# Broadcast rows, saved node states and summed attributes of a graph network moved by two or four DMA engines instead of up to sixteen

## The chip, the cores and the metric

The kernel runs on one core of a Trainium2 chip. The metric is the device time of one execution in microseconds; lower is better. The core has TensorE (PE, with its weight loads PEld), VectorE (DVE), ScalarE (ACT), GpSimd (POOL) and SyncE (SP). SP, ACT and POOL also issue transfers, and all transfers are carried by the same 16 DMA engines.

## The reference

12,500 nodes with 128 features and 200,000 edges pass through two graph networks. `x` enters a gated message layer, is added and normalised; the result passes through three layers of a second network, which sum over a node's edges the neighbour's features and the edge's encoded attributes, and it is added and normalised again.

```python
# layer 0: messages by destination, then a GRU
src_h = h[src] @ W_msg.T + b_msg
msg = src_h + edge_embed[clip(edge_type)]
messages = segment_sum(msg, dst)
x = layernorm(x + gru(messages, h))
# layers 1 to 3: the edges by source, and their attributes
ee = ea @ enc_w + enc_b
agg = segment_sum(concat(x[ei[1]], ee), ei[0])
h = relu(batchnorm(agg @ w1 + b1)) @ w2 + b2
# at the end
x = layernorm(x + h)
```

## The kernel before

**Preparation (0 to about 1250 us).** The edges are sorted twice on chip by two keys, and lists of places are made. Nothing of the change is used there except two writes of summed attributes.

**Four layers.** Nodes are split into NB = 98 blocks of P = 128. `layer(i, pace)` loops over the 98 output blocks `o`. For every block there is a row of slots: 32 slots for each of the 98 other blocks (CW = 3136 numbers in bfloat16), where each number says which of the 128 nodes of that other block belongs to the slot. Layers 0 and 1 use the whole row. Layers 2 and 3 use the first 72 blocks of it (IC*SL = 2304 numbers) and fetch the other rows by indirect gathers.

One block `o` goes through these steps:

- `slots_of` (L1507) loads the row into the tile `inr`, the same row into every one of the 128 partitions, with one DMA from SP. In layers 0 and 1 one row is loaded at a time (784 KB into SBUF); in layers 2 and 3 two rows (1152 KB). There is one buffer for `inr`, so the next load waits until the last block of the tile has been compared.
- `one_hots` makes two one-hot operands on DVE: `g` from `inr` (L1519), and `s` from the columns of the edges (L1524, four pieces). It runs one block ahead; `g` and `s` have two buffers each.
- TensorE picks rows with `g` (L1615), ACT copies them out of PSUM as `e` (L1621, L1624; DVE takes a third in layers 0 and 1, L1622), and TensorE adds them up with `s` into `acc` (L1565; gathered rows by L1570). `acc` has one buffer.
- `finish` adds `acc` in three parts to `s` on DVE (L1581 to L1583), which frees `acc`; for every two blocks `gru` (layer 0) or `gin` (layers 1 to 3) does the dense part, with L1462 on PE and L1467 on DVE (L1477 in layer 3).

The orders of the instructions on DVE, ACT and PE inside the layers are chosen by a scheduler when the program is built, and are then fixed: every engine runs its list in order. POOL's list is written by hand.

**Attributes.** `attributes` runs beside layers 0 and 1. For each block POOL issues 17 indirect gathers of 128 rows of 64 bytes (L718). `add_up` then copies the gathered tile on ACT (L738) and DVE (L739), which wait for the last of the 17. Summed attributes of seven blocks are written to DRAM as `eaT` (102 rows, L777), and `gin` reads them back as `cT` (L1433). The normalised output of layer 0 is written to DRAM as `x1` (L1357) and read back as `xx` in layer 3 (L1436).

**Rows in DRAM.** `Slots.decode` writes, during layer 0, `sl` into `inrow0` (the rows for layer 0) and `dl` into `inrow1` (the rows for layers 1 to 3). The program's access patterns for the loads before are 128 partitions on both sides:

```python
inrow = [dram(f"inrow{i}", (NB, n), BF16) for i, n in enumerate((CW, CW))]
inr = inr.rearrange("p (b c) -> p b c", c=n)
nc.sync.dma_start(inr, inrow[a][None, o:o + per, :n].to_broadcast([P, per, n]))
```

Of the kernel before, what the change touches and what calls it, by code (L numbers as in the profile page):

```python
# [9 lines left out]
BF16 = mybir.dt.bfloat16  # L10
# [8 lines left out]
H = 128  # L19
# [4 lines left out]
P = 128  # L24
NB = -(-N // P)
NPAD = NB * P
NW = NB + 2
H3 = 3 * H
SL = 32
CW = NB * SL  # L30
# [17 lines left out]
IC = 72  # L48
# [25 lines left out]
E6 = 6 * EA  # L74
# [14 lines left out]
def gnn_kernel(ctx: ExitStack, tc: tile.TileContext, x, xx, src, dst, ea, et, w_msg, w_ihT, w_hhT, b_msg,  # L89
# [4 lines left out]
    def dram(name, shape, dtype=F32):  # L94
        return nc.dram_tensor(name, shape, dtype, kind="Internal").ap()
# [4 lines left out]
    tables = [dram(f"table{i}", (P * NW, H3), BF16) for i in range(4)]  # L100
    ovf = [dram("ovf0", (P * NW, H + NTX))] + [dram(f"ovf{i}", (P * NW, H)) for i in (1, 2, 3)]
    ovfe = dram("ovfe", (P * NW, EA))
    x1d = dram("x1", (P, NB, H))

    def by_node(t, b0, n):

        return t.rearrange("(p b) f -> p b f", b=NW)[:, b0:b0 + n, :]

    inrow = [dram(f"inrow{i}", (NB, n), BF16) for i, n in enumerate((CW, CW))]
    outrow0 = dram("outrow0", (NB, CW), BF16)  # L110
    typerow = dram("typerow", (NB, CW), BF16)
    eaTd = dram("eaT", (E6, NPAD), BF16)

    const = ctx.enter_context(tc.tile_pool(name="const", bufs=1))
    psa = ctx.enter_context(tc.tile_pool(name="psa", bufs=1, space=PSUM))
# [250 lines left out]
    XC = 7  # L366
# [361 lines left out]
    def add_up(b, at):  # L728
        if b % XC == 0:
            owns.append(owp.tile([P, XC, EA], F32, name="own"))  # L730
            nc.sync.dma_start(owns[-1], by_node(ovfe, b, XC))
        own = owns[-1][:, b % XC, :]
        oh = eop.tile([P, P, WC], BF16, name="eoh")
        a3 = attr3[b % 2]
        for f0 in range(0, P, P // 2):

            if f0 == 0:
                A.copy(a3[:, :, 1:EA], at)  # L738
                V.tensor_sub(at, at, a3[:, :, 1:EA])  # L739
            else:  # L740
                A.copy(a3[:, :, EA:EA + DE], at)
                V.tensor_sub(a3[:, :, EA + DE:], at, a3[:, :, EA:EA + DE])
            V.tensor_tensor(oh[:, f0:f0 + P // 2, :], iotas[:, f0:f0 + P // 2, :WC],  # L743
                            slcol[:, b, None, :].to_broadcast([P, P // 2, WC]), op=OP.is_equal)
            yield
        early = sorting[-1]
        ps = psa.tile([P, 512], F32, name="acc") if early else psd.tile([P, 512], F32, name="d")
        for t in range(WN):
            T.matmul(ps[:, :EW], oh[:, :, t], a3[:, t, :], start=(t == 0), stop=(t == WN - 1))  # L749
        if early:  # L750
            yield
        V.tensor_add(own, own, ps[:, :EA])
        V.tensor_add(own[:, 1:], own[:, 1:], ps[:, EA:EA + DE])
        V.tensor_add(own[:, 1:], own[:, 1:], ps[:, EA + DE:EW])
        yield
        if early:
            yield
            yield
        if b % XC < XC - 1:
            return  # L760
        own = owns[-1]
        own6 = ow6.tile([P, XC, 6, EA], BF16, name="own6")
        times = lambda n: own[:, :, None, :].to_broadcast([P, XC, n, EA])
        V.tensor_copy(own6[:, :, 0:3, :], times(3))
        V.tensor_sub(own, own, own6[:, :, 0, :])
        yield
        V.tensor_copy(own6[:, :, 3:5, :], times(2))
        V.tensor_sub(own6[:, :, 5, :], own, own6[:, :, 3, :])
        yield
        pt = psa.tile([P, 1024], BF16, name="acc") if early else psd.tile([P, 1024], BF16, name="d")  # L770
        for k in range(XC):
            T.transpose(pt[:E6, k * P:(k + 1) * P], own6[:, k, :, :].rearrange("p a b -> p (a b)"), identb)
        if early:
            yield
        eT = ow6.tile([E6, XC * P], BF16, name="ownT")
        A.copy(eT, pt[:E6, :XC * P])
        nc.sync.dma_start(eaTd[:, (b - XC + 1) * P:(b + 1) * P], eT)  # L777
        summed.extend(range(b - XC + 1, b + 1))
        yield

# [278 lines left out]
    class Slots:  # L1059
# [15 lines left out]
        def decode(self, c):  # L1075

            if c >= CHUNKS:
                return
            b0, n = c * CB, min(CB, NB - c * CB)
            cells, bs, m = self.cells.pop(c), slice(b0, b0 + n), n * SL  # L1080
            ci = cells.bitcast(I32)[:, :m]
            tile_of = lambda name, d=BF16, pool=self.pool: pool.tile([NB, CB * SL], d, name=name)
            valid, ty, sm, dm = (tile_of(x) for x in ("valid", "ty", "sm", "dm"))
            sl, dl = (tile_of(x, pool=self.two) for x in ("sl", "dl"))
            fi = tile_of("fi", I32)
            as3 = lambda t: t[:, :m].rearrange("p (b s) -> p b s", s=SL)
            by_dst = lambda d: d.rearrange("d (s k) -> s d k", k=SL)
            V.tensor_tensor(as3(valid), iota[:NB, None, :SL].to_broadcast([NB, n, SL]),
                            cnt[:, bs, None].to_broadcast([NB, n, SL]), op=OP.is_lt)

            def field(to, shift, mask):
                V.tensor_scalar(fi[:, :m], ci, shift, mask, op0=OP.logical_shift_right, op1=OP.bitwise_and)
                V.tensor_scalar(to[:, :m], fi[:, :m], sgn[:NB], off[mask][:NB], op0=OP.mult, op1=OP.add)

            field(sl, 11, 127)
            nc.sync.dma_start(by_dst(inrow[0])[:, bs, :], as3(sl))
            yield
            field(dl, 4, 127)
            V.scalar_tensor_tensor(dm[:, :m], valid[:, :m], -200.0, dl[:, :m], op0=OP.mult, op1=OP.add)
            field(ty, 0, 15)  # L1100
            nc.sync.dma_start(inrow[1][:, b0 * SL:(b0 + n) * SL], dl[:, :m])
            V.scalar_tensor_tensor(sm[:, :m], valid[:, :m], -200.0, sl[:, :m], op0=OP.mult, op1=OP.add)
            yield
            ps = psd.tile([P, 512], F32, name="d")
            for k in range(n):
                for x, t in enumerate((dm, ty)):
                    for r in range(4):
                        T.matmul(ps[r * SL:(r + 1) * SL, (x * CB + k) * NTL:(x * CB + k + 1) * NTL],
                                 t[:, k * SL:(k + 1) * SL], sel[:, r, :], start=True, stop=True, skip_group_check=True)
                T.matmul(ps[k * SL:(k + 1) * SL, 256:256 + NB], sm[:, k * SL:(k + 1) * SL], identb[:NB, :NB],  # L1110
                         start=True, stop=True, skip_group_check=True)
            for x, to in enumerate((outcol[0], typecol)):
                A.copy(to[:, bs, :NTL], ps[:, x * CB * NTL:(x * CB + n) * NTL].rearrange("p (b t) -> p b t", b=n))
            m = n * SL
            A.copy(outcol[1][:m, :, CELL + c], ps[:m, 256:256 + NB])
            yield
# [220 lines left out]
    def layernorm(y, b0, n, final):  # L1337
        st = lnp.tile([P, GL, 6], F32, name="ln_st")
        mv = lnp.tile([P, GL, 2], F32, name="ln_mv")
        for k in range(n):  # L1340
            V.bn_stats(st[:, k, :], y[:, k, :])
            V.bn_aggr(mv[:, k, :], st[:, k, :])
            if k % 4 == 3:
                yield
        rstd = lnp.tile([P, GL], F32, name="ln_r")
        rsqrt(rstd[:, :n], mv[:, :n, 1], [P, n], lnp)
        yield
        for k in range(n):
            V.tensor_scalar(y[:, k, :], y[:, k, :], mv[:, k, 0:1], rstd[:, k:k + 1],
                            op0=OP.subtract, op1=OP.mult)  # L1350
            if k % 2:
                if not final:
                    split3(y[:, k - 1:k + 1, :], 1, b0 + k - 1, k == n - 1)
                yield
        if not final:
            nc.sync.dma_start(by_node(ovf[1], b0, n), y[:, :n, :])
        nc.sync.dma_start((out if final else x1d)[:, b0:b0 + n, :], y[:, :n, :])  # L1357

    group = {}

# [64 lines left out]
    def gin(i, b0, s):  # L1425
        yield
        k4 = b0 % 4
        if k4 == 0:
            m = min(4, NB - b0)
            while len(summed) < b0 + m:  # L1430
                next(attr)
            four["eT"] = dq.tile([E6, 4 * P], BF16, name="cT")
            nc.sync.dma_start(four["eT"][:, :m * P], eaTd[:, b0 * P:(b0 + m) * P])  # L1433
            if i == 3:
                four["xx"] = dq.tile([P, 2, 2, 2 * H], F32, name="xx")
                nc.sync.dma_start(four["xx"][:, 0].rearrange("p a (b f) -> p (a b) f", b=2)[:, :m, :], x1d[:, b0:b0 + m, :])  # L1436
            else:
                four["o"] = dq.tile([P, 4, H], F32, name="n")
        eT = four["eT"][:, k4 * P:(k4 + 2) * P]
# [45 lines left out]
    def layer(i, pace):  # L1485
# [16 lines left out]
        def slots_of(o):  # L1502

            n = nb * SL
            inr = rp.tile([P, 2 * IC * SL], BF16, name="inr")[:, :per * n]
            inr = inr.rearrange("p (b c) -> p b c", c=n)
            nc.sync.dma_start(inr, inrow[a][None, o:o + per, :n].to_broadcast([P, per, n]))  # L1507
            inrs.append(inr)

        def one_hots(o):  # L1510

# [197 lines left out]
```

## Time and profile before

| | |
|---|---|
| median of 3 runs | 6211.23 us (6205.5 to 6216.66) |
| the profiled execution | 6211.41 us |
| its span, first to last instruction | 6209.6 us |
| mean granted TensorE clock | 0.888 |
| PE busy | 4981.5 us (80%) |
| DVE, ACT, POOL busy | 3730.2, 3722.9, 3328.5 us |
| row loads: layers 0 and 1 | 196 of 784 KB |
| row loads: layers 2 and 3 | 98 of 1152 KB |

The stretches of the span are: preparation to 1250 us, layer 0 to about 2880, layer 1 to 4235, layer 2 to 5210, layer 3 to the end. A line number such as L1507 is a line of the kernel before; in the changed kernel the same lines stand 9 to 11 lines further down. Busy shares are means over a stretch; what a change is worth is read from what ends the waits there.

### The profile page before, as it was taken

How to read it: one execution, taken by the hardware profiler on the slowest of the kernel's cores; microseconds unless marked ns; L12 is line 12 of the kernel's file. 1: busy time of each engine (PE TensorE's matmuls, PEld its weight loads, DVE VectorE, ACT ScalarE, POOL GpSimd, SP SyncE). 2: the span in 40 equal slices, each digit the busy share in tenths (PEclk: the TensorE clock that was granted, in tenths of full speed). 3: DMA queues.
4: the chain of work that ended last, by engine and by line, in shares of the span. 5: the costliest groups of instructions: out<-in, count | busy, mean ns of one | idle time of the engine just before them, and what ended most of it. 6: DMA issues, size and time to landing. Idle time of an engine off the chain costs nothing. (4 is left out here: it accounts for less than half of the span.)

```text
span 6209.6 us, 129682 instructions
## 1 busy us (share of the span) xinstructions
PE 4981.5 (80%) x50669; PEld 2867.1 (46%) x50669; DVE 3730.2 (60%) x9301; ACT 3722.9 (60%) x5300; POOL 3328.5 (54%) x4109
## 2 busy tenths in 40 slices
PE   3872431148888888898899999958999998999999
PEld 3872121124444444443455555534555555555555
DVE  9977777656766766666566656634444443444444
ACT  7770221025665656565677777736777776777776
POOL 1004777356665666665566666663555553655553
PEclk9755555568999999999999999979999999999999
DMA  1001210022222322224222223214444445444443
GB/s 71 22 1 32 84 38 8 11 53 77 82 81 80 96 79 84 81 86 146 83 89 93 91 88 98 89 44 163 143 139 139 139 139 164 145 137 137 136 137 103
DMA packets 278104, 575.34 MB, mean 93 GB/s; under 512 B 74269, under 2 KB 169897, under 8 KB 276835
## 3 DMA queue, kind: packets, MB, share of 16 engines
q1 hardware_dynamic: 158946, 416.84, 19.2%
q0 software_dynamic: 105920, 116.17, 8.1%
q10 hardware_dynamic: 12616, 33.99, 1.6%
q8 instruction: 397, 6.50, 0.4%
q14 instruction: 225, 1.84, 0.1%
HBM read 478.02 MB, written 88.73 MB: 91 GB/s over the span
## 5 line engine op out<-in xcount | busy, mean ns | idle before, releaser
L1624 ACT CAST e<-g 128x1152 bf16<-128x1152 f32 (+1 forms) x2156 | 2260.1, 1061 | 746.7 <-PE g L1615 668.6
L1615 PE MATMUL g<-x,g 128*32 128x384 bf16 x33320 | 1954.8, 335 | 156.1 <-ACT e L1624 80.4
L718 POOL DMA_INDIRECT eat<-in_ea,eidcol x1666 | 1768.9, 1062 | 543.2 <-issue 448.9
L1565 PE MATMUL acc<-e,s 128*128 128x384 bf16 (+3 forms) x8428 | 1978.4, 349 | 89.5 <-DVE s L1583 58.6
L1565 PEld LDWEIGHTS <-s 128*128 128x128 bf16 (+1 forms) x8428 | 1090.2, 155 | 869.8 <-issue 643.8
L1541 POOL DMA_INDIRECT x<-table,rowcol x980 | 974.3, 994 | 918.5 <-PE acc L1570 728.0
L1615 PEld LDWEIGHTS <-g 128*32 128x32 bf16 x33320 | 698.4, 96 | 1077.4 <-issue 851.6
L1621 ACT CAST e<-g 128x768 bf16<-128x768 f32 x784 | 627.8, 801 | 414.8 <-PE g L1615 299.9
L1524 DVE TENSOR_TENSOR s<-iotas,outcol 128x832 bf16<-128x832 bf16 (+1 forms) x1568 | 873.5, 568 | 1.0 <-PE acc L1565 1.0
L1643 POOL COPY token<-e 1x1 bf16<-1x1 bf16 x1274 | 383.2, 301 | 694.9 <-ACT e L1624 444.1
L1622 DVE CAST e<-g 128x384 bf16<-128x384 f32 x784 | 434.4, 554 | 514.9 <-ACT e L1621 508.8
L1519 DVE TENSOR_SCALAR g<-inr,pidx 128x3136 bf16<-128x3136 bf16 (+1 forms) x392 | 370.0, 944 | 573.7 <-PE g L1615 550.5
L557 PE MATMUL acc<-ot,oa 125*98 125x101 bf16 x1600 | 295.8, 359 | 125.9 <-ACT ot L538 85.7
L557 PEld LDWEIGHTS <-oa 125*98 125x98 bf16 x1600 | 291.9, 277 | 129.0 <-issue 82.0
L1581 DVE TENSOR_TENSOR s<-s,acc 128x128 f32<-128x128 f32 x392 | 112.2, 286 | 383.6 <-PE acc L1565 378.4
L538 ACT ACTIVATE ot<-dbb,bias 125x160 bf16<-125x160 bf16 (+2 forms) x1078 | 332.2, 403 | 16.6 <-PE acc L557 15.9
L1570 PE MATMUL acc<-x,s 128*128 128x384 bf16 x980 | 330.8, 338 | 8.7 <-DMA x<-table,rowcol 8.7
L749 PEld LDWEIGHTS <-eoh 128*128 128x128 bf16 x1666 | 117.0, 162 | 307.5 <-DVE eoh L743 240.8
L799 POOL IOTA num<- 98x2176 uint16 x1 | 1.9, 1946 | 459.4 <-DMA sortedB<-keyB 459.4
L738 ACT CAST attr<-eat 128x272 bf16<-128x272 f32 x98 | 43.1, 440 | 324.4 <-DMA eat<-in_ea,eidcol 318.1
L1454 ACT ACTIVATE gates<-d,shift,scale 128x256 f32<-128x256 f32 x294 | 150.0, 560 | 110.7 <-PE d L1452 110.5
L1627 DVE TENSOR_TENSOR e<-iota,typecol 128x30 bf16<-128x30 f32 (+1 forms) x882 | 152.1, 178 | 99.1 <-POOL token L1643 71.6
(421 smaller groups left out, 4817.0 us busy)
## 6 DMA issues: line engine op xcount, KB each, us to landing
inr<-inrow SPq DMA_DIRECT2D x196, 784.0 KB
inr<-inrow SPq DMA_DIRECT2D x98, 1152.0 KB
table<-x SPq DMA_DIRECT2D x72, 384.0 KB
eat<-in_ea,eidcol POOLq DMA_INDIRECT x1666
s<-ovf SPq DMA_DIRECT2D x72, 256.0 KB
x<-table,rowcol POOLq DMA_INDIRECT x980
x<-table ACTq DMA_DIRECT2D x19, 672.0 KB
xx<-in_xx SPq DMA_DIRECT2D x24, 512.0 KB
```

The lines of the kernel that those rows point to most:

```text
L538: A.activation(self.ot[j % 2][:, b, :ENDS[j] - c0], dbb[:, c0:ENDS[j]], AF.Sign, bias=self.bias[:, b:b + 1], scale=-1.0)
L557: T.matmul(cps[:NB, :NB + NQ - 1], self.oa[c // HC][:, :, c % HC], self.ot[j % 2][:, :, c - (ENDS[j - 1] if j else 0)], start=(c == 0), st ...
L718: G.indirect_dma_start(out=at[:, t, :], out_offset=None, in_=ea, in_offset=bass.IndirectOffsetOnAxis(ap=eidcol[:, b, t:t + 1], axis=0))
L1519: V.tensor_scalar(g[:, :nb * SL], inr[:, o % per, :nb * SL], pidx, None, op0=OP.is_equal)
L1524: V.tensor_tensor(st[:, f0:f0 + P // 4, :], iotas[:, f0:f0 + P // 4, :tw], outcol[a][:, o, None, c0:c0 + tw].to_broadcast([P, P // 4, tw]) ...
L1541: G.indirect_dma_start(out=place(asked), out_offset=None, in_=tables[i], in_offset=bass.IndirectOffsetOnAxis(ap=rowcol[:, o, p.kept + j:p. ...
L1565: T.matmul(sums[o][:, :wid], st[:m, :, cell + t], e[:m, j, :wid], start=(t == 0), stop=(t == tiles - 1), skip_group_check=True)
L1615: T.matmul(pg[c * SL:(c + 1) * SL, j, :H3], g[:, b * SL:(b + 1) * SL], piece(X, b), start=True, stop=True)
L1621: A.copy(e[:, :2, :H3], pg[:, :2, :H3])
L1622: V.tensor_copy(e[:, 2, :H3], pg[:, 2, :H3])
L1624: A.copy(e[:m, :n, :H3], pg[:m, :n, :H3])
L1643: G.tensor_copy(token, e[0:1, 0, 0:1])
```

## The change

The rows of slots for layers 1 and for layers 2 and 3 get DRAM tensors of their own: `inrow1` with 2 blocks of 49 rows and `inrow2` with 7 blocks of 14 rows of only 2304 numbers, each block followed by an unused row. `dl` is written to both where both need it, which adds 18 small writes. The row loads name their source as four copies of 32 copies in place of 128 copies. In layers 2 and 3 the two rows of a load now lie next to each other, so that one partition receives 9216 bytes in a piece instead of two pieces of 4608. `x1` lies in DRAM as 4 blocks of 32 rows with an unused row after each, `eaT` as 2 blocks of 51 rows likewise. The instructions of PE, DVE, ACT and POOL keep their number and their order; only SP has 18 more.

The access patterns that result, as step and count, destination and source:

```
inr, layers 0 and 1   before [4608,128][1,3136]          <- [0,128][1,3136]
                      after  [4608,128][1,1][1,3136]     <- [0,4][0,32][1,3136]
inr, layers 2 and 3   before [4608,128][2304,2][1,2304]  <- [0,128][3136,2][1,2304]
                      after  [4608,128][1,1][1,4608]     <- [0,4][0,32][1,4608]
cT                    before [512,102][1,512]            <- [12544,102][1,512]
                      after  [512,102][1,1][1,512]       <- [652288,2][12544,51][1,512]
```

```diff
-    x1d = dram("x1", (P, NB, H))
+    x1d = dram("x1", (4, P // 4 + 1, NB * H))
-    inrow = [dram(f"inrow{i}", (NB, n), BF16) for i, n in enumerate((CW, CW))]
+    inrow0 = dram("inrow0", (NB, CW), BF16)
+    inrow = [dram(f"inrow{i}", (h, NB // h + 1, n), BF16) for i, h, n in ((1, 2, CW), (2, 7, IC * SL))]
+
+    def slot_rows(i, o, n):
+        if i == 0:
+            return inrow0[o:o + n, :]
+        t = inrow[i > 1]
+        o, p = divmod(o, NB // t.shape[0])
+        return t[o, p:p + n, :]
...
-    eaTd = dram("eaT", (E6, NPAD), BF16)
+    eaTd = dram("eaT", (2, E6 // 2 + 1, NPAD), BF16)
...
-        nc.sync.dma_start(eaTd[:, (b - XC + 1) * P:(b + 1) * P], eT)
+        nc.sync.dma_start(eaTd[:, :-1, (b - XC + 1) * P:(b + 1) * P], eT)
...
-            nc.sync.dma_start(inrow[1][:, b0 * SL:(b0 + n) * SL], dl[:, :m])
+            for t in inrow:
+                if b0 * SL < t.shape[2]:
+                    nc.sync.dma_start(t[:, :-1, b0 * SL:(b0 + n) * SL], dl[:, :m])
...
-        nc.sync.dma_start((out if final else x1d)[:, b0:b0 + n, :], y[:, :n, :])
+        nc.sync.dma_start(out[:, b0:b0 + n, :] if final else x1d[:, :-1, b0 * H:(b0 + n) * H], y[:, :n, :])
...
-            nc.sync.dma_start(four["eT"][:, :m * P], eaTd[:, b0 * P:(b0 + m) * P])
+            nc.sync.dma_start(four["eT"][:, :m * P], eaTd[:, :-1, b0 * P:(b0 + m) * P])
...
-            inr = inr.rearrange("p (b c) -> p b c", c=n)
-            nc.sync.dma_start(inr, inrow[a][None, o:o + per, :n].to_broadcast([P, per, n]))
-            inrs.append(inr)
+            rows = slot_rows(i, o, per).rearrange("(x b) c -> x (b c)", x=1)
+            nc.sync.dma_start(inr, rows[:, None, :].to_broadcast([4, P // 4, per * n]))
+            inrs.append(inr.rearrange("p (b c) -> p b c", c=n))
```

## The prediction

> **What bounds the kernel now.** I read the page first: PE is busy 80% of the span, and in the chain that ended last DMA holds 1%. So there is hardly any waiting for transfers to win back. The row loads are the largest group of transfers:
>
> ```profile
> inr<-inrow SPq DMA_DIRECT2D x196, 784.0 KB
> inr<-inrow SPq DMA_DIRECT2D x98, 1152.0 KB
> ```
>
> Next the windows by stage, and two narrow ones around a pause of PE in layer 0 (columns: window, then busy us of PE, PEld, DVE, ACT, POOL, then PEclk, DMA share, GB/s):
>
> ```profile
> 4235.00:5210.00 975.00, 928.74 (x10169) 543.41 (x10166) 423.21 (x1038) 725.98 (x793) 487.27 (x505) 0.99 0.44 144
> 2055.00:2060.00 5.00, 2.85 (x31) 1.19 (x28) 2.77 (x11) 0.80 (x1) 4.37 (x7) 0.98 0.08 13
> 2060.00:2065.00 5.00, 5.00 (x23) 1.78 (x23) 2.52 (x9) 2.18 (x3) 3.28 (x6) 0.68 0.34 73
> ```
>
> Layer 2 (and 3 likewise) is bound by PE at full clock. The other two rows show what a pause costs: PE pauses for 2.15 us in the first, and in the second its granted clock is 0.68. The clock records put it at 0.5 for 3.41 us there; between 1400 and 4000 us most pauses of 2 us and more are followed by such a piece, or by one of 6.83 us, and about half of those of 1.5 to 2 us.
>
> Then the timeline of one load in layer 2 (start, length, engine, line, tiles, and in brackets the idle time and what ended it):
>
> ```profile
> 4709.20 0.37 SPq L1507 DMA_DIRECT2D inr<-inrow  x1
> 4718.26 0.82 DVE L1519 TENSOR_SCALAR g<-inr,pidx 128x2304 bf16<-128x2304 bf16 x1 [3.36 <-PE g L1615]
> 4721.36 0.42 DVE L1467 TENSOR_TENSOR n<-d,wset 128x256 f32<-128x256 f32 x1 [2.27 <-PE d L1462]
> 4722.77 0.29 DVE L1581 TENSOR_TENSOR s<-s,acc 128x128 f32<-128x128 f32 x1 [0.66 <-PE acc L1565]
> 4723.97 0.28 DVE L1583 TENSOR_TENSOR s<-s,acc 128x128 f32<-128x128 f32 x1
> 4724.31 0.88 PE L1565 MATMUL acc<-e,s 128*128 128x384 bf16 x4 [0.44 <-DVE s L1583]
> ```
>
> The load has 9.06 us until DVE would use it. `g` itself is not urgent, but DVE works in order, and behind `g` stand L1467 and L1581 to L1583, which free `acc`, and PE already waits 0.44 us for them. The slack after `g` is 2.27 + 0.66 = 2.93 us, of which about 0.15 is lost because L1469 and the issue of L1581 follow L1467 closely. So a load may take 9.06 + 2.8 = about 11.85 us before PE is late; beyond that PE is late by all of it. Layer 3 has the same offsets (9.06, 2.27, then 0.25 and 0.6).
>
> Last the transfers of layer 1 in a window inside one load (packets, MB, share of 16 engines, and the issues in it):
>
> ```profile
> DMA packets 108, 0.68 MB, mean 339 GB/s; under 512 B 0, under 2 KB 0, under 8 KB 108
> q1 hardware_dynamic: 108, 0.68, 91.2%
> eat<-in_ea,eidcol POOLq DMA_INDIRECT x2
> ```
>
> 108 packets of 6272 bytes took 0.912 x 16 x 2.0 us: 0.27 us each on one engine (0.24 in the steady part). And POOL's gathers have no packet in these 2 us, though one was issued at 3460.09: a load's eight rows pass an engine in one go, and gathers wait behind them.
>
> **What the change costs, part by part.** Whether it confines a transfer: `cT`, 102 rows, has 17 packets of 1024 bytes on each of six engines in the packet records, so the engine count follows the outer size (6 divides 102). A source of 4 x 32 against 128 partitions then gives four engines, eaT's 2 x 51 gives two. [...]
>
> *Loads of layers 2 and 3.* Per engine 32 rows of 9216 bytes, at 0.24 to 0.27 us for 6272: 32 x 0.35 to 0.40 = 11.2 to 12.7 us. Now it is 16 x 0.178 = 2.85 us, and the load takes 5.2 us at least and 5.9 in the median from issue to its full semaphore count, so 2.3 to 3.1 us lie around the data. Together 13.5 to 15.8; I take 13.9, near the low end, because the steady rate rules in long runs. PE is late by 13.9 - 11.85 = 2.0 us per load. The pause then is 2.0 + 0.44 = 2.5 us, longer than the 2.15 above, so the clock halves for 3.4 us and 1.7 us of work is lost; I count this 9 times in 10: 1.5 us. 97 loads x 3.5 = **340 us**. By the low end (late by 1.0, clock kept) it is 100 us; by the high end (late by 3.9, pieces of 6.83 us) 97 x 7.3 = 710. [...]
>
> *Gathers in layers 2 and 3* wait up to 11 us on the four engines. They are issued 15 ahead of use, three blocks or 29 us, so PE's L1570 hides it. `s`, `cT` and `xx` queue behind a load on the same engines; they are issued 18 us and more before use, `cT` costs 51 x 0.045 = 2.3 us on two engines, `xx` 2.5 us on four: hidden, since a load, these and the gathers fill about 90% of 19.4 us and the period grows.
>
> *Layers 0 and 1.* A load needs 32 x 0.24 = 7.7 us on four engines, with 1.9 around it 9.5; DVE uses it 10.2 us later or more in nine of ten cases of layer 1, 12 in layer 0: hidden. Not hidden is the attribute gather behind it. ACT (L738) waits for the 17th gather, with what this costs PE:
>
> ```profile
> 2710.55 0.43 ACT L738 CAST attr<-eat 128x272 bf16<-128x272 f32 x1 [6.65 <-DMA eat<-in_ea,eidcol]
> 2711.02 0.44 DVE L739 TENSOR_TENSOR eat<-eat,attr 128x272 f32<-128x272 f32 x1 [4.60 <-ACT attr L738]
> 2711.29 0.39 PE L1405 MATMUL d<-ew,cT 60*128 60x512 bf16 x1 [3.28 <-ACT cT L1396]
> ```
>
> I laid a busy stretch from 1.0 to 8.65 us after each load's issue over the 76 last gathers of these layers (arrival 1.9 us after issue): 41 fall into one, and ACT would wait 121 us more in all. PE lost half of ACT's wait above (3.28 of 6.65); I take two thirds, 80 us, and 20 new pauses with a slower clock, 20 x 1.7 = 35: **115 us**. If gathers slip in between rows it is 20, if PE loses all and the clock twice that, 190. [...] No load before has more than 16 such rows on an engine, so no row decides it, though 32 pieces of 512 bytes (`s`, L1579) also let hardly a gather packet through.
>
> *Starts of layers.* The load that ends the chain at the start of layer 3 (17.09 us, behind `x<-table`) and its like in layers 1 and 2 get longer by the data: 5.8 + 8.4 + 8.4 = about **25 us**. *Small things.* Writes of `x1` (32 x 0.156 = 5 us on four engines) stand 3 to 12 us ahead of the next load, two of them too close: 5 us. 18 more writes on SP at 0.3 us each lie in its waits. `eaT` on two engines, 3.6 us, 14 times, is read far later. Together **10 us**.
>
> Sum: 340 + 115 + 25 + 10 = 490 on 6211.4 us of the profiled execution (span 6209.6; the median of the runs is 0.2 lower): 6700 us.
>
> **The rivals.**
>
> *Faster: the twelve freed engines.* Gathers no longer meet a load on all 16 engines, and if the four engines change between queues row by row, a gather waits under 0.4 us. ACT's wait for gathers in layers 0 and 1 is 159 us, of which perhaps 40 are collisions. For the sum to be a gain the big loads must also land within 11.85 us, that is 32 rows in 9 us, 33 GB/s per engine against 26 in the records. Then about 6180 us. I give it 8%.
>
> *No confinement.* If the zero steps of 4 x 32 are joined to 128 on the way, loads stay on 16 engines and only `cT`, `eaT`, `x1` and rows of 9216 bytes differ: 6211 us. The writes with gaps can't be joined, but are hidden. 4%.
>
> *Four engines full.* If rows of 9216 bytes go slower, or gathers break into each load, engines 0 to 3 are full in layers 2 and 3 and gathers come late too: late by 6 us per load with the clock down for 6.83 us, 97 x 9 = 900, with the rest about 7250 us. 10%.
>
> **How the numbers follow.** My case has 78% and reaches from 6211 + 100 + 20 = 6330 to the sum of its middle high ends, 6211 + 600 + 190 + 50 = about 7050; the range is that, 6330 to 7050, leaving out the two rivals near zero and most of the full engines. A measurement of this kernel tells 0.2% (12 us) from no change. Slower by more: 78 + 10% = 88%; the same 4%; faster 8%.
>
> **What would show it.** Right: `g` (L1519, then L1530) in layers 2 and 3 waits for the DMA of `inr` some 5 us, every second time; a period of two blocks of 22 to 24 us in place of 19.4; PE's wait for L1583 about 2.5 us; PEclk near 0.9 in layers 2 and 3 in place of 0.99; ACT's L738 waiting over 200 us for gathers. Wrong: no wait of `g` (loads on 16 engines or faster rows), a clock that stays at 0.99 (340 becomes 194), or L738 unchanged.

## The result, and the profile after

The changed kernel takes 8201.9 us (median of 4 runs, 8179.0 to 8217.4) against 6212.0 us for the kernel before, measured beside it: **1.320 times as long, 95% interval 1.317 to 1.324**. The prediction said slower, 6700 us; the loss is 1990 us in place of 490. The profiled execution after has a span of 8205.6 us and a mean TensorE clock of 0.801 (before 6209.6 us and 0.888).

First the page: the TensorE clock in 40 slices, and the shares of the chain that ended last by engine. Before, DMA held 1% of that chain and PE 25%.

```profile
PEclk9555556888988888898999878878888778888778
...
DMA 42%; PE 10%; DVE 5%; issue 2%; POOL 1%; ACT 1%; SPq 0%; DVEq 0%; ACTq 0%; POOLq 0%
```

The stages, each from its first `g`, before and after: layer 0 1628.5 and 1917.8 us, layer 1 1361.5 and 1696.1, layer 2 969.6 and 1651.5, layer 3 987.1 and 1670.3. So 1365 us of the loss lie in the two layers with the large loads. The window of layer 2 (busy us of PE, PEld, DVE, ACT, POOL, then PEclk, DMA share, GB/s):

```profile
4890.00:6530.00 1640.00, 1022.01 (x10119) 550.36 (x10116) 406.71 (x1020) 722.68 (x784) 475.06 (x494) 0.81 0.36 84
```

The row of before had about as many matmuls in 975 us, PEclk 0.99. Here PE is busy 62% of the time at a clock of 0.81. One load of that layer in the timeline:

```profile
5079.07 33.62 SPq L1518 DMA_DIRECT2D inr<-inrow  x2
5102.44 0.82 DVE L1530 TENSOR_SCALAR g<-inr,pidx 128x2304 bf16<-128x2304 bf16 x1 [17.67 <-DMA inr<-inrow]
5103.18 0.42 DVE L1478 TENSOR_TENSOR n<-d,wset 128x256 f32<-128x256 f32 x1
5103.84 0.28 DVE L1592 TENSOR_TENSOR s<-s,acc 128x128 f32<-128x128 f32 x1
5105.04 0.28 DVE L1594 TENSOR_TENSOR s<-s,acc 128x128 f32<-128x128 f32 x1
5105.38 2.14 PE L1576 MATMUL acc<-e,s 128*128 128x384 bf16 x6 [11.63 <-DVE s L1594]
```

The load is issued at 5079.07 (the row counts two issues, so its length is not that of one), and DVE can start `g` only at 5102.44, 23.4 us later; before it was ready in time for 9.06. DVE sat idle for 17.67 us, and the three instructions behind `g` that free `acc` (L1592 to L1594) kept PE waiting for 11.63 us. The chain of waits tells the same in order of time (start, length, what):

```profile
5078.22 0.83 DVE g L1530
...
5079.07 23.27 DMA inr<-inrow
...
5102.44 0.06 DVE g L1530
...
5105.04 0.29 DVE s L1594
...
5105.38 2.14 PE acc L1576 x6
```

From issue to the full semaphore the loads of layers 2 and 3 take 24.0 us in the median (5.9 before), those of layers 0 and 1 14.4 us (4.1 before). Each load's semaphore now gets 4 updates from the transfer in place of 16, that of a `cT` read 2 in place of the 6 it got on six engines, so the load is on four engines, as predicted. The 9216-byte packets (one row into one partition) took 545 ns in the median; the 4608-byte ones before took 178.

### The profile page after: what moved, and what is told of

Same layout as the page of the kernel before. It is cut to its first block, busy times and chain, and to the rows that moved or that the text cites. A ratio compares the mean times of both kernels' runs of the same rounds, so it can differ in the third digit from the quotient of the medians.

```text
span 8205.6 us, 129696 instructions
## 1 busy us (share of the span) xinstructions
PE 5354.2 (65%) x50669; PEld 2923.9 (36%) x50669; DVE 3708.4 (45%) x9301; ACT 3727.8 (45%) x5300; POOL 3292.4 (40%) x4109
## 4 chain that ended last, share of the span: by engine, by line
DMA 42%; PE 10%; DVE 5%; issue 2%; POOL 1%; ACT 1%; SPq 0%; DVEq 0%; ACTq 0%; POOLq 0%
DMA inr<-inrow 39%; PE acc L1576 5%; PE g L1626 4%; DVE g L1530 2%; DMA eat<-in_ea,eidcol 2%; DVE s L1535 1%; POOL eat L727 1%; PE acc L1581 1%; DMA xx<-x 1%; PE d L1473 0%; DVE s L1592 0%; DVE s L1594 0%; DVE s L1593 0%; ACT e L1635 0%; DVE n L1478 0%
## 5 line engine op out<-in xcount | busy, mean ns | idle before, releaser
L1576 PE MATMUL acc<-e,s 128*128 128x384 bf16 (+3 forms) x8428 | 2171.4, 376 | 1292.7 <-DVE s L1594 1209.1
L1626 PE MATMUL g<-x,g 128*32 128x384 bf16 x33320 | 2080.0, 354 | 424.6 <-DVE e L1633 269.9
L727 POOL DMA_INDIRECT eat<-in_ea,eidcol x1666 | 1792.5, 1076 | 596.5 <-issue 504.9
L1576 PEld LDWEIGHTS <-s 128*128 128x128 bf16 (+1 forms) x8428 | 1104.2, 156 | 2204.1 <-DVE s L1594 1249.2
L1552 POOL DMA_INDIRECT x<-table,rowcol x980 | 952.4, 972 | 2291.9 <-PE acc L1581 2015.9
L1626 PEld LDWEIGHTS <-g 128*32 128x32 bf16 x33320 | 726.4, 99 | 1485.9 <-issue 1252.1
L1654 POOL COPY token<-e 1x1 bf16<-1x1 bf16 x1274 | 343.2, 269 | 1270.4 <-ACT e L1635 829.2
L1581 PE MATMUL acc<-x,s 128*128 128x384 bf16 x980 | 359.7, 367 | 22.1 <-DMA x<-table,rowcol 22.1
L1341 ACT CAST x<-n 128x256 bf16<-128x256 f32 x98 | 39.8, 406 | 564.1 <-DVE n L1480 562.0
L1592 DVE TENSOR_TENSOR s<-s,acc 128x128 f32<-128x128 f32 x392 | 110.7, 282 | 316.0 <-PE acc L1576 312.0
L335 DVE TENSOR_TENSOR keyA<-keyA 128x1024 f32<-128x1024 f32 (+1 forms) x178 | 191.1, 1074 | 15.8 <-ACT keyA L351 12.7
```

The costliest lines, as they stand in the source:

```text
L727: G.indirect_dma_start(out=at[:, t, :], out_offset=None, in_=ea, in_offset=bass.IndirectOffsetOnAxis(ap=eidcol[:, b, t:t + 1], axis=0))
L1552: G.indirect_dma_start(out=place(asked), out_offset=None, in_=tables[i], in_offset=bass.IndirectOffsetOnAxis(ap=rowcol[:, o, p.kept + j:p. ...
L1576: T.matmul(sums[o][:, :wid], st[:m, :, cell + t], e[:m, j, :wid], start=(t == 0), stop=(t == tiles - 1), skip_group_check=True)
L1581: T.matmul(sums[o][:, :H3], st[:, :, row + j], place(o * rt + j), start=False, stop=False, skip_group_check=True)
L1626: T.matmul(pg[c * SL:(c + 1) * SL, j, :H3], g[:, b * SL:(b + 1) * SL], piece(X, b), start=True, stop=True)
L1654: G.tensor_copy(token, e[0:1, 0, 0:1])
```

## The experiments

The kernel before took 6208 to 6215 us beside these runs, except where said. Three theories stand in the expectations of the first runs: **A**, two engines that write partitions 32 apart in SBUF at the same time share a way in and slow each other (with 32 partitions per engine, engines 0 and 1 stand 32 apart in every row, and so do 2 and 3); **B**, gathers break into the loads; **C**, four engines that read the same DRAM row disturb each other.

**The rows alone.** A kernel that leaves out the whole computation: broadcasts of one row into `inr`, one at a time, each followed by a DVE copy that waits for it.

```
for r in range(5):
    [128] of 9216 B on 16 engines; [4, 32]; [4, 32] of 6272 B; [8, 16];
    [2, 32] into partitions 0..63; [2, 32] into 32..95; [4, 8] into 0..31;
    four pieces [4, 8] into 0.., 32.., 64.., 96..; [1, 32]; [4, 32] of distinct rows
```

> Computes nothing of the reference: row loads alone, each waited for before the next, no gather, no other engine at work, five times each. Theory A (two engines that write partitions 32 apart at the same time share a way into SBUF and get half the rate each): one row of 9216 bytes to 128 partitions on 16 engines 5 us; on four engines with 32 partitions each 23 to 25 us; rows of 6272 bytes so 14 to 17 us; on eight engines with 16 each 12 to 14 us (7.5 if nothing is shared); two engines on partitions 0 to 63 23 to 25 us, the same two engines on partitions 32 to 95 12 to 14 us; one engine, 32 partitions, 12 to 14 us; four pieces of 32 partitions, each over the same four engines, 13 to 15 us; rows with gaps from DRAM in place of one row like the broadcast, 23 to 25 us. Theory B (gathers break into the loads in the kernel): alone, four engines need 13 to 14 us for 9216 bytes and 9.5 us for 6272, and the two places of two engines are alike, 12 to 14 us. Theory C (four engines that read the same DRAM row at the same time hinder each other): the broadcast needs 24 us, rows with gaps 13 to 14 us, both places of two engines alike, and four pieces as long as one.

The timeline of one round; the number in brackets is DVE's wait, which is the time of the load before it. A case such as [4, 32] names four shares of 32 copies, so four engines with 32 partitions each. In order: 16 engines, [4, 32], [4, 32] of 6272 bytes, [8, 16], two engines on partitions 0 to 63, the same on 32 to 95, four pieces, and [4, 32] of distinct rows.

```profile
177.19 0.16 DVE L131 COPY seen<-inr 128x1 bf16<-128x1 bf16 x1 [5.77 <-DMA inr<-rows]
197.90 0.16 DVE L131 COPY seen<-inr 128x1 bf16<-128x1 bf16 x1 [20.55 <-DMA inr<-rows]
211.08 0.16 DVE L131 COPY seen<-inr 128x1 bf16<-128x1 bf16 x1 [13.03 <-DMA inr<-rows]
224.32 0.16 DVE L131 COPY seen<-inr 128x1 bf16<-128x1 bf16 x1 [13.08 <-DMA inr<-rows]
245.77 0.16 DVE L131 COPY seen<-inr 128x1 bf16<-128x1 bf16 x1 [21.30 <-DMA inr<-rows]
259.55 0.16 DVE L131 COPY seen<-inr 128x1 bf16<-128x1 bf16 x1 [13.63 <-DMA inr<-rows]
...
280.57 0.16 DVE L131 COPY seen<-inr 128x1 bf16<-128x1 bf16 x1 [14.75 <-DMA inr<-rows]
...
303.56 0.16 DVE L131 COPY seen<-inr 128x1 bf16<-128x1 bf16 x1 [19.00 <-DMA inr<-gaps]
```

The fifth and sixth lines settle the main point: two engines, 32 rows each, the same source row, nothing else at work, and only the place differs: 21.3 us on partitions 0 to 63, 13.6 us on 32 to 95 (20.4 to 21.3 and 13.6 to 14.0 in the five rounds). Four engines with 32 partitions each take as long as the bad pair (20.5 us), and all four report their end between 17 and 21 us, so both pairs are slow. The same rows on the same four engines in four pieces of 32 partitions take 14.75. Theory C falls: distinct rows take 19.0 us (18.6 to 20.4 in the five rounds), where it had 13 to 14. B can't explain a loss without gathers. A was too dark: all its cases with engines 32 apart except [8, 16] came out 1 to 4 us below the range expected. The bad pair's packets take 18.7 us from first to last (median of the rounds), 18.7 / 32 = 0.58 us per row; the good one's take 11.8 us, 0.37 per row, so a load is not twice as long. A single packet often is: in the round shown 41 of the bad pair's 64 packets took 0.63 us or more, but 9 took 0.37 or less; of the good pair's, 56 took 0.35. The bad pair's two engines start their rows 0.01 us apart at first and up to 0.4 us apart later; that this lets some rows pass undisturbed is likely and was not tried. The single-engine case did not test what it was meant to: it came out on 16 engines (3.8 us).

**Which partitions disturb each other.** The same kernel with other places.

```
for k, d, p in ((2, 64, 0), (2, 16, 0), (2, 16, 32), (4, 16, 0), (4, 16, 32), (2, 32, 0), (2, 32, 32), (4, 32, 0)):
    [k, d] rows into partitions p .. p + k*d - 1
```

> Computes nothing of the reference: broadcasts of one row of 9216 bytes alone, each waited for, on two engines with 64, 16 or 32 partitions each, or four with 16 or 32, at different first partitions, five times each. If partitions 32 apart share a way into SBUF within 0 to 63 and within 64 to 127, and no others: two with 64 each (0 to 127) 24 to 25 us, which is 0.35 us a row; two with 16 each, at 0 or at 32, 7.2 to 7.8 us; four with 16 each at 0 (two pairs 32 apart within 0 to 63) 11 to 12.5 us; four with 16 each at 32 (pairs 32 and 64, 48 and 80) 7.2 to 8 us; two and four with 32 as before, 20.5, 13.6 and 20.3. If any two engines that write at the same partition modulo 32 disturb each other, 64 each 45 us and four with 16 at 32 some 12.

The timeline of the second round, for [2, 64] at 0, [4, 16] at 0 and [4, 16] at 32:

```profile
181.73 0.16 DVE L123 COPY seen<-inr 128x1 bf16<-128x1 bf16 x1 [24.50 <-DMA inr<-rows]
...
210.39 0.16 DVE L123 COPY seen<-inr 128x1 bf16<-128x1 bf16 x1 [11.86 <-DMA inr<-rows]
219.46 0.16 DVE L123 COPY seen<-inr 128x1 bf16<-128x1 bf16 x1 [8.91 <-DMA inr<-rows]
```

Engines 64 partitions apart did not disturb each other (64 rows in 24.5 us, 0.36 us each), nor did those 16 apart (8.0 and 8.3 us for [2, 16], where 7.2 to 7.8 was expected). Engines 32 partitions apart did when both lay within 0 to 63 (11.86 us) or both within 64 to 127 (the second pair of [4, 32] above, done only after 17 to 21 us), and not across the middle (8.91). An engine that no other disturbed moved 9216 bytes in 0.36 us, 26 GB/s. Of the bad pair's packets, 0.66 us in the median of the round shown, two together are 28 GB/s, little more than that one engine alone; its whole load, with the rows that passed quickly, comes to 31 GB/s, so its engines did not hold each other up all the time. That the two share a way into SBUF stays theory A's reading: the runs show which pairs are slow and by how much, not why.

**Four pieces in the kernel.**

```
-            nc.sync.dma_start(inr, rows[:, None, :].to_broadcast([4, P // 4, per * n]))
+            for q in range(0, P, P // 4):
+                nc.sync.dma_start(inr[q:q + P // 4], rows[:, None, :].to_broadcast([4, P // 16, per * n]))
```

> The changed kernel, each load of rows as four DMAs of 32 partitions, each over the same four engines with 8 partitions each: the same engines, bytes and rows per engine, but no two engines write partitions 32 apart at the same time. Theory A: loads land 13 to 15 us after issue in layers 2 and 3 and 9 to 11 us in layers 0 and 1; by the prediction's sum some 6700 us, 6450 to 6950. Theories B and C: loads land at 24 and 14 us as now, 8100 to 8300 us.

6564.8 us (1.057, 1.055 to 1.059): the same four engines, bytes and rows per engine, and 1637 us of the 1990 are gone. The time is in theory A's range. The loads land 17.2 and 17.0 us after the first of their four issues in layers 2 and 3, later than the 13 to 15 expected, and at 10.9 in layers 0 and 1. The time gained overstates what the pairs 32 apart cost: the scheduler also put `g` elsewhere in DVE's order, where it is less urgent, so layer 2 loses next to nothing (979 us). Two more runs take that apart.

**The same pieces on 16 engines.** PE, DVE and ACT have exactly the order of the run above.

```
+            for q in range(0, P, P // 4):
+                nc.sync.dma_start(inr[q:q + P // 4], rows.to_broadcast([P // 4, per * n]))
```

> The control of the four pieces: each load as four DMAs of 32 partitions, as there, but each piece over all 16 engines; the instructions of PE, DVE and ACT stand in the same order as with the four pieces on four engines. If that order and the number of DMAs cost nothing, 6210 to 6290 us and the 353 us that the four pieces on four engines lost are the four engines'. If they cost, 6400 to 6560, and the four engines without the shared way into SBUF cost less than 150.

6323.8 us (1.018, 1.016 to 1.020). Between the two expectations: order, pieces and the other edits cost 109 us, and four engines without such pairs 6564.8 - 6323.8 = 241 us, of which 57, 34, 16 and 134 in layers 0 to 3. In layer 3 DVE waits 53.3 us for rows on four engines and not on 16, and longer for `xx`, which stands behind the rows on the same four engines. That wait on 16 engines, us in total, times, longest:

```profile
DVE xx L1487 <- DMA xx<-x: 37.1, 24, 2.4
```

On four it is 118.7 us in as many waits, 81.6 more. The control is not free of slow rows either: its 9216-byte packets took 674 ns in the median, longer than the 545 of the changed kernel. But with 16 engines at work its loads land 8.5 and 9.2 us after the first issue in layers 2 and 3, before the 11.85 us at which PE would be late. Why these packets are slow was not tried.

**No pairs 32 apart, `g` at its place.** Layers 2 and 3 alone, in three DMAs.

```
+            for q, m in ((0, P),) if i < 2 else ((0, 32), (32, 64), (96, 32)):
+                nc.sync.dma_start(inr[q:q + m], rows[:, None, :].to_broadcast([4, m // 4, per * n]))
```

> The changed kernel, layers 2 and 3 alone with each load in three DMAs over the same four engines: partitions 0 to 31, 32 to 95, 96 to 127, in which no two engines share a way into SBUF at the same time. On DVE g stands at its place of the changed kernel, but for one instruction (L1478 goes ahead of it). If the shared way is what the prediction missed: landing at about 17 us, as with the four pieces, of which 3 us are the gathers; late by 17.0 - 11.85 = 5.2 us, with the clock 6.9, period 26.3 in place of 33.4 us: 8202 - 97 x 7.1 = 7510 us, 7400 to 7620. If it is not, 8150 to 8250.

Beside this run the kernel before took 6483 us (1.170, 1.168 to 1.173), 4% more than beside the others, and nothing measured here shows why. So its 7581 us, though within the range expected, are not set beside the others. Within its trace: the 9216-byte packets took 353 ns in place of 545, loads land at 17.2 us, and the period of two blocks is 26.1 us, where 26.3 was expected. The timeline (L numbers are one higher):

```profile
5513.47 0.82 DVE L1531 TENSOR_SCALAR g<-inr,pidx 128x2304 bf16<-128x2304 bf16 x1 [4.55 <-DMA inr<-inrow]
...
5515.94 2.15 PE L1577 MATMUL acc<-e,s 128*128 128x384 bf16 x6 [4.12 <-DVE s L1595]
```

PE's wait is 4.12 us in place of 11.63.

**Without the gathers of layers 2 and 3.** After the first that fill their places they are left out; blocks then use the rows that lie there.

```
-            if asked == NB * rt:
+            if asked == rb * XC:
```

> The changed kernel without the gathers of x in layers 2 and 3, after the first that fill their places: the blocks use the rows that lie there, so what is added for those edges is not the reference's. Theory A (shared way into SBUF, and gathers only the rest): loads land at 20.5 us as alone in place of 24.0, so each is late by 8.7 in place of 12.1 us: 8202 - 97 x 3.4 = 7870 us, 7780 to 7960. Theory B (the gathers that break into the loads cost all above 13.9 us): landing 13.9 us, 7100 to 7300. If gathers take nothing from the loads, 24 us and 8200.

7969.5 us (1.284, 1.282 to 1.286), 10 us above theory A's range and 232 us less than with them; loads land at 21.2 us. So gathers lengthen a load, but by 2.8 us, not by the 10 us of theory B. That they slip in between its rows is shown by their semaphores in the changed kernel. A gather's semaphore gets 16 updates, one from each engine. Of the gathers issued within 1 us after a load of layer 2, twelve engines have reported 5.6 us after the load's issue, and the last four, which carry the load, after 9.6 to 10.7 us (medians), while the load lands at 24.0 us. In the kernel before, the last engine reported at 6.0 us, 0.2 us after the load (5.8): there the gather waited for the load's end.

**Asked two blocks ahead.** In layers 2 and 3 one row per load, into either half of `inr`; PE, DVE and ACT keep their order.

```
-        per = 1 if i < 2 else 2
+        per, both = 1, rp.tile([P, 2 * IC * SL], BF16, name="inr")
...
+            inr = (both if i < 2 else both[:, o % 2 * n:])[:, :n]
...
+            if o + 1 + i // 2 < NB:
+                slots_of(o + 1 + i // 2)
```

> The changed kernel, in layers 2 and 3 one row of 4608 bytes per load into either half of inr, asked for two blocks ahead: the same bytes over the same four engines, but twice the time until the load is used; PE, DVE and ACT keep their order. If it is the time from issue to landing that PE waits for, and the engines have room (two rows take them 20 to 22.5 us), the period of two blocks falls from 33.4 to 20 to 22.5 us: 8202 - 97 x (33.4 - 21.3) = 7030 us, 6880 to 7160. If the four engines are full whatever is asked ahead (gathers and others beside the rows), the period stays at 24 to 30 us: 7250 to 7900.

7059.4 us (1.136, 1.134 to 1.138), within the range. Same bytes on the same four engines with the pairs still 32 apart, and layer 2 is back at a period of 19.4 us (991 us in all). So the engines were not full: what PE waited for was the time from issue to landing. In layer 3 (1204 us) the next in the queue shows:

```profile
DVE xx L1487 <- DMA xx<-x: 228.8, 24, 12.2
```

**Half of the layers each.** Loads of layers 2 and 3 back on 16 engines, then those of layers 0 and 1.

```
-            nc.sync.dma_start(inr, rows[:, None, :].to_broadcast([4, P // 4, per * n]))
+            if i >= 2:        # second run: i < 2
+                nc.sync.dma_start(inr, rows.to_broadcast([P, per * n]))
+            else:
+                nc.sync.dma_start(inr, rows[:, None, :].to_broadcast([4, P // 4, per * n]))
```

> The changed kernel with the loads of layers 2 and 3 back on 16 engines, those of layers 0 and 1 on four. If the stages' costs add up: 8202 - 665 - 683 = 6854 us, 6800 to 6900, with layers 2 and 3 at 960 and 954 us again. If the rows of 9216 bytes or the other edits (x1, attributes' sums) have a part in the late layers, above 6900.

6792.1 us (1.094, 1.092 to 1.096), 62 us under the sum and just below the range, with layers 2 and 3 at 969 and 989 us, as in the kernel before (970 and 987).

> The changed kernel with the loads of layers 0 and 1 back on 16 engines, those of layers 2 and 3 on four. If the costs add up: 8202 - 287 - 322 = 7593 us, 7540 to 7640. If part of the cost of layers 0 and 1 is of the writes of attributes' sums and x1 on fewer engines, more: up to 7750.

7626.4 us (1.229, 1.227 to 1.231), within the range.

**All loads on 16 engines, the rest of the change kept.**

```
-            nc.sync.dma_start(inr, rows[:, None, :].to_broadcast([4, P // 4, per * n]))
+            nc.sync.dma_start(inr, rows.to_broadcast([P, per * n]))
```

> The changed kernel with all loads of rows back on 16 engines; the writes and reads of x1 on four engines, of the attributes' sums on two, the rows one after the other in DRAM and the 18 more writes stay. If these are as small as the prediction's 10 us, 6210 to 6240 us. The kernel with only layers 2 and 3 on four engines lost some 37 us in layer 0 and 28 in layer 1; if those are of the remaining edits, 6260 to 6290.

6276.0 us (1.010, 1.008 to 1.012): 61 us. With this as the base the loads of layers 2 and 3 cost 7626 - 6276 = 1350 us, those of layers 0 and 1 6792 - 6276 = 516; the remaining 1990 - 1350 - 516 - 61 = 63 us come only when both are on four engines.

**x1 alone, and the rows' tables alone**, each put into the kernel before.

```
+    x1d = dram("x1", (4, P // 4 + 1, NB * H))
...
+        nc.sync.dma_start(out[:, b0:b0 + n, :] if final else x1d[:, :-1, b0 * H:(b0 + n) * H], y[:, :n, :])
...
```

> The kernel before with the change to x1 alone: its writes in layer 0 and its reads in layer 3 on four engines. All loads on 16 engines with the other edits kept cost 61 us, 43 of them in layer 0 and 17 by block 14 of layer 1. x1 is written in layer 0 only: if it is the cause, 6250 to 6275 us; if not, 6205 to 6225.

6248.9 us (1.006, 1.005 to 1.008): 39 us, 36 of them in layer 0. A write of x1 now takes 11 us from issue to its full semaphore, 4.4 in the median before. The `table` writes of the next blocks follow, and ACT now waits for them in layer 0, which it did not before:

```profile
ACT x L1330 <- DMA table<-x: 28.0, 5, 6.2
```

> The kernel before with the change to the slots' rows in DRAM alone: two tables with a row of gap in place of one, 18 more writes in layer 0, and a load of layers 2 and 3 as one row of 9216 bytes; all loads on 16 engines. If the 18 writes in layer 0 are the cause of the 61 us, 6250 to 6275; if not, 6205 to 6225. What neither this nor x1 explains is of the attributes' sums on two engines.

6207.8 us (0.9998, 0.999 to 1.001): no difference, 18 more writes and rows of 9216 bytes on 16 engines included. That leaves some 22 us of the 61, by difference, for the attributes' sums on two engines, which were not tried alone.

## Why the prediction was wrong

The direction was right, and so was the chain from a late load through `g` and `acc` to PE. The price of a row was not, and two things that the prediction put at nothing cost time: gathers that break into a load, and the loads of layers 0 and 1.

**Confinement**: right. The count followed the outer size where that was 2, 4 or 8 (2, 4 and 8 updates of the semaphore for [2, 32], [4, 32] and [8, 16]), but not where it was 1 (16 updates for [1, 32]).

**Loads of layers 2 and 3** (predicted 340, measured about 1350): the step that failed is "32 x 0.35 to 0.40 = 11.2 to 12.7 us". A row's time was carried over from 16 engines, as if it belonged to the engine alone. It did where no other engine wrote 32 partitions away in the same half of 64: 0.36 to 0.37 us per row, and 13.6 us for the load, beside the 13.9 predicted. With 32 partitions per engine both pairs stand 32 apart in every row, and a row took 0.58 us. The 24.0 us are made of: about 14.7 without such pairs (four pieces, alone), 5.8 for the pairs (20.5 alone), 0.7 for other traffic (by difference) and 2.8 for the gathers. In the kernel, taking the pairs apart is worth 24.0 - 17.2 = 6.8 us.

What follows the landing was right. Late by landing less 11.85, the prediction's 1.7 us for the clock, on a period of 19.4:

| | landing us | 19.4 + late + 1.7 | measured period |
|---|---|---|---|
| no pairs 32 apart | 17.2 | 26.5 | 26.1 |
| without gathers | 21.2 | 30.5 | 30.7 |
| changed kernel | 24.0 | 33.3 | 33.4 |

So 97 x 13.9 = 1348 us come from the predicted rule with another landing. The granted clock did fall with PE's pauses, as the row at 2060 had said: the six matmuls after the pause took 2.14 us (the L1576 row above), 1.20 before. Its size fits only nearly. In layers 2 and 3 the clock is at 0.5 in pieces of 10.24 or 13.65 us and not of 3.41, most of each inside the pause (65% of a piece in the median), and PE's busy time per period in layer 2 rose from 18.7 to 20.8 us, 2.1 in place of 1.7.

The signs named ahead came in kind and not in size: `g` waits for the rows every second time, but 18 us and not 5, and PEclk is 0.81 and not 0.9.

**Gathers in layers 2 and 3**: PE does not wait for them, as predicted. What was left out is the other direction: they lengthen each load by 2.8 us, 232 us in all. How much of it is time on the four engines and how much is writing beside them was not separated. The statement that a load's rows pass an engine in one go held for runs of eight or sixteen rows and not for 32 on four engines.

**Layers 0 and 1** (predicted 115 and 6 at the start of layer 1, measured 516): "hidden" was wrong, and the gathers' part was right in its number only. A load needs 14.4 us in place of 9.5, past the 10.2 that layer 1 allows. Waits of layer 1, the gathers' before the change, then rows and gathers after it:

```profile
ACT attr L738 <- DMA eat<-in_ea,eidcol: 83.0, 25, 19.9
...
DVE g L1530 <- DMA inr<-inrow: 269.1, 68, 12.8
ACT attr L747 <- DMA eat<-in_ea,eidcol: 146.8, 25, 20.0
```

`g` did not wait for rows in layer 1 before; in layer 0 it now waits another 84.4 us. ACT's wait for the attribute gathers in both layers rose from 76.1 + 83.0 to 140.8 + 146.8 us, by 128.5 where 121 had been worked out. That is luck. The 121 rest on gathers that wait for the end of a load, 8.65 us after its issue. In the trace an attribute gather issued within 1 us after a load of layer 1 is complete 8.0 us after the load's issue (median; 4.8 before), while the load lands at 14.4: the gather gets through about half of the rows, and the rows are slower. Without the pairs (four pieces) loads land at 10.9 us, ACT waits 242.6 us, 49 more than with the same pieces on 16 engines, `g` waits 15 us in all, and layers 0 and 1 cost 91 us more than on 16 engines, under the 121 predicted. How the 516 us split between the two waits was not measured by itself.

**Small things** (predicted 10, measured 61): x1 was priced at 5 us per write and counted only where a load stood close behind. It takes 11, reading SBUF with the same spacing of 32 partitions, and the queue behind it also holds the `table` writes. That its cause is again the spacing was not tried by itself.

**The rivals and the range.** "Four engines full" named both ingredients (slower rows, gathers breaking in) but not the size, nor the reason: the engines had room, as the run two blocks ahead shows. The range failed with the row price: its upper part took 15.8 us as the slowest load, from rows that had all been measured with 16 engines at work, and no reason excluded a price that depends on who writes next door. Its low end was also out of step with the sum: 13.5 us, the shortest load there, is late by 1.65 us and not by 1.0, which is 160 us and not 100. The faster rival had nothing in it: ACT's waits for gathers grew, and no load landed earlier.

## What to carry to other kernels

When a change moves a transfer to fewer engines, look also at which partitions are then written at the same moment. Lay the engines' shares out partition by partition and look for pairs 32 apart within the same half of 64: here such a pair took 0.58 us per 9216-byte row in place of 0.37. In this kernel the confined transfer lost far less when it was cut so that no pair stood there, or when it was asked for one use earlier; and behind a longer transfer, look through everything that its queue and engines hold next (`xx`, `table`, the gathers), not only for its own reader.

## What the runs showed of the hardware

- Two engines, 32 rows of 9216 bytes each, alone: 21.3 us into partitions 0 to 63, 13.6 us into 32 to 95. Eight engines with 16 partitions each, which also stand in pairs, took 13.1 us, hardly less than two engines with 32 that don't stand in pairs.
- A leading 1 in a broadcast of [1, 32] did not confine the transfer: it went over 16 engines (16 updates of its semaphore) in 3.8 us.
- Gathers slipped in between the rows of a load of 32 rows per engine: issued within 1 us after it, they were complete 10.7 us after its issue in layer 2, with the load landing at 24.0, and 8.0 of 14.4 in layer 1. Before, with 16 and 8 rows per engine, they were complete 0.2 and 0.7 us after the load.
